# Loading x and the gate weights of a recurrence in two parts of two chunk rows each

## The chip, the cores and the metric

The kernel runs on one core of a Trainium2 chip. The metric is the device time of one execution in microseconds. Three executions of the kernel before took 1618.48, 1618.99 and 1623.41 us; their median is 1618.99 us. One further execution, taken by the hardware profiler, took 1615.84 us, and all rows below are from it.

## The reference

`x` has 16 batch rows of 512 steps and 512 features; four layers are added to it one after the other, each as `x = x + layer(x, cond)`. All is float32.

- Layer 0 is a wavelet transform with a gate on every coefficient. Since the gate is the same for all of them, `v + inverse(gate * forward(v))` is `v * (1 + gate)`, and with the outer sum x becomes `x * (2 + gate)`. The gate depends on `cond` alone.
- Layer 1 is a recurrence over the 512 steps: `h = tanh(x_t @ Wx + b + h @ Wh)`, with `h` of 512 features for 16 batch rows. The next x is `x + h`.
- Layer 2 has a forget gate, an input gate and a candidate, each a product of x with a 512 x 512 matrix; the two gates go through a sigmoid and are divided by their sum, and two running sums and products over the steps follow.
- Layer 3 is a product of x with `base + A B`, where the factors A and B (rank 8 for each batch row) are made from `cond` through a layer norm, a gelu layer and a layer of 8192 columns. With the outer sum the matrix is `base + 2 * identity + A B`.

```python
h_next = jnp.tanh(xw_t + h_prev @ Wh)
forget_gate = jax.nn.sigmoid(jnp.einsum('bsd,hd->bsh', input_seq, W_f) + b_f)
layer = base_layer[None, :, :] + jnp.einsum('bdr,bkr->bdk', x_a, x_b)
out = jnp.einsum('btc,bco->bto', x, layer)
```

## The kernel before

The features lie on 128 partitions in `KC` = 4 chunks. The kernel has three parts: an opening (gate of layer 0, first loads), the recurrence, and a loop over the 16 batch rows for layers 2 and 3.

The recurrence runs over `NBLK` = 64 blocks `n` of `T` = 8 steps `s`. Its order on TensorE (PE), ScalarE (ACT), VectorE (DVE) and SyncE (SP) is the order in which the code is written; nothing is rearranged. In each step

- PE multiplies the last `h` with `wh_sb` (16 products, `accumulate`, L417), and then does other products that do not depend on `h`: the x products of the next block (`inputs`), a part of the rank factors of layer 3 (`layer_part`, L380), or a part of an early gate of layer 2 (`early_gate`, L465);
- ACT takes the tanh of four column groups (L609), and DVE transposes each of them into the next `h` (L610);
- DVE then does one smaller thing: in steps 0 to 3 it multiplies a quarter of the x of block `n + 2` by the gate of layer 0 (`gated`, L178: each quarter takes some steps and all four chunk rows of the loaded tile `xb`), in steps 4 to 7 it adds `h` to x (L622). One piece of an early gate (L489 to L500) may follow;
- ACT issues transfers behind the four tanh: in even steps the second half of a row of the layer 3 weights (`rest`, up to about block 16), in steps 1 and 3 of blocks 0 to 7 one load of a gate weight or of `base`, and in step 5 the x of block `n + 3` (L159) into the single buffer `xb`;
- after that, in steps 7, 0 and 2, ACT copies the bias into a PSUM bank of a coming block (`begin`, L214), and the sigmoid of an early gate may follow.

The x of block `n + 3`, loaded in block `n`, is first read by DVE in step 0 of block `n + 1`. The first early gate begins in block 2; `SETS` and `PARTS` set the order of the others, in the order of weight chunks 2, 3, 0, 1. `base_sb` is read at the end of block 12, where DVE adds twice the identity to its diagonal blocks (L666, four operations), and then only after the recurrence. SP issues the first halves of the layer 3 weights, the stores of the early gates and the rank factors. At the end of a block `end_layer` adds the bias of a rank factor (L395) and stores it; in step 0 of block 1 it makes the hidden layer of layer 3 instead (DVE L399 and L400, then a gelu on ACT, L401).

A DMA issue of SP or ACT also waits until an earlier transfer, some eight before it, is complete, since the semaphores of the transfers are used in turn.

Of the kernel before, what the change touches and what calls it, by code (L numbers as in the profile page):

```python
# [35 lines left out]
P = 128  # L36
B, S, D = 16, 512, 512
KC = D // P
R = 8

T = 8
NBLK = S // T
# [3 lines left out]
G = len(PAIRS)  # L46
# [37 lines left out]
def kernel(  # L84
# [21 lines left out]
    nc = tc.nc  # L106
    PSUM = bass.MemoryType.PSUM

    def chunks(w):
        return w.rearrange("(k p) n -> p k n", p=P)  # L110
# [12 lines left out]
    wf_sb = keep.tile([P, KC, D], F32)  # L123
    wi_sb = keep.tile([P, KC, D], F32)
    wc_sb = keep.tile([P, KC, D], F32)
    base_sb = keep.tile([P, KC, D], F32)
# [13 lines left out]
    xpool = rnn.enter_context(tc.tile_pool(name="xpool", bufs=3))  # L140
# [13 lines left out]

    bias_sb = rw.tile([P, KC, BP], F32)

    def load_x(n, pool=xpool, tag="xb", engine=nc.sync):
        xb = pool.tile([P, KC, T, B], F32, tag=tag, name=f"xb_{n}", bufs=1)
        engine.dma_start(  # L159
            out=xb.rearrange("p k t b -> p k (t b)"),  # L160
            in_=xT[:, n * T : (n + 1) * T, :].rearrange("(k p) t b -> p k (t b)", p=P),
        )
        return xb

    H = G // 2
# [14 lines left out]
    def new_x1(n):  # L180
        return xpool.tile([P, KC, G, 2, B], F32, tag="x1", name=f"x1_{n}")
# [14 lines left out]
    def new_bank(n, i, name):  # L196

        return ps_r[i][n % 2].tile([P, G, P], F32, tag="pre", name=f"{name}_{n}_{i}")
# [25 lines left out]
    with tc.tile_pool(name="ps_pre", bufs=1, space=PSUM) as ps_pre:  # L224
# [15 lines left out]
        xb = load_x(2)  # L240
# [108 lines left out]


    rest = []
    chunk_sb = []

    def load_chunk():
# [14 lines left out]
    def layer_part(i, k):  # L369

        if k == 0:
            layer_part.ps = ps_p.tile([P, P], F32, tag="pf", name=f"pf_{i}")
            if i:
                which, r = LAYERS[i]
                layer_part.bias = w2pool.tile([P, P], F32, tag="b2", name=f"b2_{i}", bufs=2)
                row = (bias_a, b2b)[which][r].rearrange("(j o p) -> j o p", j=KC, o=1)
                nc.sync.dma_start(out=layer_part.bias, in_=row.to_broadcast([KC, BP, P]))
        columns, src = (straight, hT3) if i else (tile_columns, aeT)
        for j in range(KC):
            nc.tensor.matmul(  # L380
                layer_part.ps[j * BP : (j + 1) * BP, :],
                src[:, k, :],
                columns(chunk_sb[i * KC + k], j),
                start=(k == 0),
                stop=(k == KC - 1),
                skip_group_check=True,
            )
        load_chunk()
# [27 lines left out]
    def accumulate(pre, g, j, lhsT, w):  # L416
        nc.tensor.matmul(  # L417
            pre[PLACE[g][0]][j * BP : (j + 1) * BP, PLACE[g][1], :],
            lhsT,
            tile_columns(w, j),  # L420
            start=False,
            stop=False,
            skip_group_check=True,
        )

    def inputs(n, i, pre):

        g, k = divmod(i, KC)
        for j in range(KC):
            accumulate(  # L430
                pre, g, j, xs[n][:, k, PAIRS[g][0] // 2].rearrange("p t b -> p (t b)"), wx_sb[:, k, :]
            )
# [122 lines left out]

    BEGINS = {T - 1: 0, 0: 1, 2: 2}

    pre, nxt = banks
    for _ in range(AHEAD):
        load_chunk()  # L560
# [4 lines left out]
    for n in range(NBLK):  # L565
        ahead = []
        if n + 2 < NBLK:
            xs.append(new_x1(n + 2))
        for s in range(T):
            odd = s % 2  # L570
            waiting = len(rest)
            g = next(i for i, pair in enumerate(PAIRS) if s in pair)
            for k in range(KC):
                for j in range(KC):
                    accumulate(pre, g, j, h_prev[:, k, :], wh_sb[:, k, :])
            if n == 0 and s < G - 1:
                for i in range((s + (s > 0)) * KC, (s + 2) * KC):
                    inputs(0, i, pre)

            if n + 1 < NBLK:  # L580
                if n == 1 and s in LATE:
                    for i in range(*LATE[s]):
                        inputs(n, i, pre)
                for i in range(*SHARE[n][s]):
                    inputs(n + 1, i, nxt)
            if s in LAYER_STEPS[n]:
                layer_part(n, LAYER_STEPS[n].index(s))
            if s in PARTS[n]:
                early_gate(made, n * T + s)
                made += 1  # L590
            if (n, s) == (NBLK - 1, T - 1):


                first_layer = [
                    new_bank(NBLK, i, "pl").rearrange("p g f -> p (g f)") for i in range(NBANK)
                ]
                first_layer.append(ps_q.tile([P, D], F32, tag="pg", name="pl_3"))
                make_layer(*first_rows, first_layer)
            a = apool.tile([P, P], F32, tag="a", name=f"a_{n}_{s}")

            h = h_out[s]
            if odd:
                turned, h_prev = h[:, :, :BP], h[:, :, B:]
            else:
                turned, h_prev = h[:, :, B:], h[:, :, :BP]
            bank, place = PLACE[g]
            for c in range(KC):
                at = slice(c * BP, (c + 1) * BP)
                nc.scalar.activation(a[:, at], pre[bank][:, place, at], AF.Tanh)  # L609
                nc.vector.transpose(turned[:, c, :], a[:, at])  # L610
            if n == 0 and s < G:

                gated(nc.vector, xs[1], x1, (0, 2, 1, 3)[s])
            if n == 0 and s == G - 1:
                opening.close()
                x2pool = ctx.enter_context(tc.tile_pool(name="x2pool", bufs=1, side="right"))
                x2 = x2pool.tile([P, KC, B, S], F32)
            if s == max(PAIRS[g]):
                t0, t1 = PAIRS[g]
                step = t1 - t0  # L620
                at = slice(n * T + t0, n * T + t1 + step // abs(step), step)
                nc.vector.tensor_tensor(  # L622
                    x2[:, :, :, at].rearrange("p k b t -> p k t b"),
                    xs[n][:, :, t0 // 2, :, :],
                    turned.rearrange("p k (t b) -> p k t b", t=2),
                    ALU.add,
                )
            elif n + 2 < NBLK:
                gated(nc.vector, xs[n + 2], xb, s)
            if (n, s) == (1, 1):  # L630

                nc.scalar.activation(probe, g2[:, 0, :1], AF.Sigmoid)
            if waiting and (odd == 0 or n == 0):
                rest.pop(0)()
            if s in (1, 3) and n < 2 * KC:


                i = 2 * n + s // 3
                if i < 3 * KC:
                    m, which = divmod(i, 3)  # L640
                    w_sb, w = ((wf_sb, wfT), (wi_sb, wiT), (wc_sb, wcT))[which]
                    j = (KC - 2, KC - 1, 0, 1)[m]
                    at = slice(j * P, (j + 1) * P)
                    nc.scalar.dma_start(out=w_sb[:, :, at], in_=chunks(w)[:, :, at])
                else:
                    k = i - 3 * KC
                    nc.scalar.dma_start(out=base_sb[:, k, :], in_=base[k * P : (k + 1) * P, :])
            if s == G + 1 and n + 3 < NBLK:
                xb = load_x(n + 3, engine=nc.scalar)
            if s in BEGINS:  # L650
                if s < T - 1 and 0 < n < NBLK - 1:
                    nxt.append(begin(n + 1, BEGINS[s]))
                elif s == T - 1 and n + 2 < NBLK:
                    ahead.append(begin(n + 2, BEGINS[s]))
            if (n, s) == (1, 0):

                end_layer(0)

            for _ in range(1 if n < NBLK - 2 else 2):
                do_pieces(n * T + s)  # L660
        if 0 < n < len(LAYERS):
            end_layer(n)
        if n == 2 * KC + 4:
            for k in range(KC):
                diag = base_sb[:, k, k * P : (k + 1) * P]
                nc.vector.scalar_tensor_tensor(diag, ident, 2.0, diag, ALU.mult, ALU.add)  # L666
        if n == FIRST - 1:
            turn_bias()
        if n == NBLK - 4:
            at = w2pool.tile([P, P], F32, tag="b2", name="at_0", bufs=2)  # L670
            bt = w2pool.tile([P, D], F32, tag="w2", name="bt_0", bufs=AHEAD)
            first_rows = load_layer(0, at, bt)
        pre, nxt = nxt, ahead
# [197 lines left out]
```

## Time and profile before

| what | value |
|---|---|
| median of three executions | 1618.99 us (1618.48 to 1623.41) |
| the profiled execution | 1615.84 us, span 1614.1 us |
| opening, to the first tanh | 16.7 us |
| recurrence with layer 3 weight loads, blocks 0 to 16 | 16.74 to 255.56, DMA share 0.48, 132 GB/s |
| recurrence, blocks 17 to 63 | 255.56 to 908.10, DMA share 0.12, 34 GB/s |
| layers 2 and 3 | 908.10 to 1614.10 |
| PE busy | 1603.6 us, 99% of the span |
| DVE / ACT / GpSimd busy | 1132.3 / 424.9 / 172.6 us |
| granted TensorE clock | 1.000 |
| x loads on ACT's queue | 61 of 256 KB, issue 0.374 to 0.412 us |
| l3w loads on ACT's queue | 64 of 128 KB |
| weight loads on ACT's queue | 12 of 256 KB for the gates, 4 of 256 KB for base |

A row of the order of time is: start in us, duration, engine, line, operation, out<-in with sizes, xcount, and in brackets how long the engine had been idle before and who released it. Rows that follow each other without a gap are merged under their count. `ACTq` and `SPq` are the sequencers, where issues of DMAs show. `PEld` is the weight load of PE. A row of the waits is: engine, what it waited with, whom it waited for, microseconds in total, number, the longest. A row of stretches is: from:to, length, then busy microseconds and instructions in brackets for PE, PEld, DVE, ACT and GpSimd, the granted clock, the mean share of the 16 DMA engines, and GB/s. PE's busy time is modelled for pipelined products, so its 99% does not mean that it works at its peak.

### The profile page before, as it was taken

The page shows a single profiled execution, that of the slowest core. Times are in us where ns is not written, and L with a number is a line of the kernel's source. Part 1 is how long each engine was busy: PE and PEld are TensorE (multiplying, and loading weights), DVE is VectorE, ACT ScalarE, POOL GpSimd, SP SyncE. Part 2 cuts the span into 40 slices and gives each one's busy share as a digit, 9 for nine tenths or more (in the row PEclk, how much of TensorE's full clock was granted, in tenths as well). Part 3 has the DMA queues.
Part 4 walks back from the last instruction along what each step waited for, and adds up shares of the span by engine and source line. Part 5 has one row for each costly group of instructions (what it writes and reads, how often), then busy time and mean ns, then how long its engine had stood idle before and what let it go on. Part 6 is the DMA issues. An engine that isn't in the chain of part 4 may idle for free.

```text
span 1614.1 us, 67901 instructions
## 1 busy us (share of the span) xinstructions
PE 1603.6 (99%) x29328; PEld 1146.0 (71%) x29328; DVE 1132.3 (70%) x3618; ACT 424.9 (26%) x2484; POOL 172.6 (11%) x145
## 2 busy tenths in 40 slices
PE   9999999999999999999999999999999999999998
PEld 6888888888888888888888655555555555555564
DVE  4555655565556666666665798888888888988887
ACT  3333333333333333333333211111111111111111
POOL 0000000000000000000000022222222222222222
PEclk9999999999999999999999999999999999999999
DMA  7554431111111111111111101111111111111111
GB/s 228 148 147 128 121 105 46 36 31 36 37 37 37 37 37 37 37 37 31 37 39 30 29 21 43 33 43 39 43 40 44 44 46 39 31 44 47 37 44 58
DMA packets 128085, 88.11 MB, mean 55 GB/s; under 512 B 22645, under 2 KB 116633, under 8 KB 127785
## 3 DMA queue, kind: packets, MB, share of 16 engines
q1 hardware_dynamic: 79152, 55.05, 11.1%
q10 hardware_dynamic: 48632, 28.73, 6.2%
q8 instruction: 229, 3.75, 1.0%
q14 instruction: 72, 0.58, 0.1%
HBM read 55.67 MB, written 28.07 MB: 52 GB/s over the span
## 4 chain that ended last, share of the span: by engine, by line
PE 96%; DVE 2%; DMA 1%; issue 0%; SPq 0%; ACT 0%; ACTq 0%; DVEq 0%
PE pre L417 41%; PE po L756 13%; PE pg L465 13%; PE pf L700 9%; PE pc L700 9%; PE pi L700 9%; PE pf L380 1%; PE pl_layer L535 1%; DVE s L718 1%; DMA wh_sb<-in_wh_dram 1%; PE pl_last L756 0%; DMA xb<-in_xT_dram 0%; DVE s L726 0%; DVE s L730 0%; PE po_last L756 0%
## 5 line engine op out<-in xcount | busy, mean ns | idle before, releaser
L417 PEld LDWEIGHTS pre<-wh_sb,h_out 128*32 128x32 f32 x16384 | 466.7, 110 | 146.6 <-DVE h_out L610 143.4
L417 PE MATMUL pre<-wh_sb,h_out 128*32 128x128 f32 x16384 | 560.6, 273 | 2.4 <-DVE h_out L610 1.1
L610 DVE STREAM_TRANSPOSE h_out<-a 128x32 f32<-128x32 f32 x2048 | 264.6, 187 | 347.4 <-ACT a L609 345.9
L609 ACT ACTIVATE a<-pre 128x32 f32<-128x32 f32 x2048 | 238.0, 203 | 573.4 <-PE pre L417 572.7
L417 PE MATMUL pre<-wx_sb,x 128*32 128x128 f32 x8192 | 285.9, 273 | 1.0 <-DMA wx_sb<-in_wx_dram 0.5
L417 PEld LDWEIGHTS pre<-wx_sb,x 128*32 128x32 f32 x8192 | 239.0, 110 | 2.1 <-DMA wx_sb<-in_wx_dram 1.5
L756 PE MATMUL po<-wx_sb,x 128*128 128x512 f32 x480 | 209.0, 592 | 0.1
L756 PEld LDWEIGHTS po<-wx_sb,x 128*128 128x128 f32 x480 | 91.0, 190 | 111.6 <-issue 105.7
L700 PE MATMUL pf<-x,wf_sb 128*128 128x352 f32 (+3 forms) x512 | 165.3, 466 | 0.3 <-DVE x L622 0.3
L700 PE MATMUL pc<-x,wc_sb 128*128 128x352 f32 (+3 forms) x512 | 163.7, 463 | 1.3 <-DVE i L722 1.3
L700 PE MATMUL pi<-x,wi_sb 128*128 128x352 f32 (+3 forms) x512 | 163.6, 462 | 0.0
L718 DVE RECIPROCAL s<-s 128x368 f32<-128x368 f32 (+2 forms) x64 | 152.2, 2378 | 2.2
L700 PEld LDWEIGHTS pf<-x,wf_sb 128*128 128x128 f32 x512 | 96.0, 190 | 68.4 <-issue 15.8
L736 POOL TENSOR_TENSOR s<-s,f 128x512 f32<-128x512 f32 x63 | 86.5, 1374 | 509.9 <-DVE s L730 504.1
L700 PEld LDWEIGHTS pc<-x,wc_sb 128*128 128x128 f32 x512 | 97.2, 190 | 57.5 <-DVE i L722 1.9
L700 PEld LDWEIGHTS pi<-x,wi_sb 128*128 128x128 f32 x512 | 97.3, 190 | 55.9
L622 DVE TENSOR_TENSOR x<-x,h_out 128x128 f32<-128x128 f32 x256 | 101.2, 395 | 18.9 <-DMA wi_sb<-in_wiT_dram 0.2
L751 ACT COPY osb<-po 128x512 f32<-128x512 f32 x60 | 35.1, 585 | 263.4 <-PE po L756 144.9
L683 POOL MEMSET zero<- 128x1 f32 x1 | 0.1, 98 | 907.5 <-DVE wx_sb L539 907.5
L717 DVE SCALAR_TENSOR_TENSOR s<-f,i 128x368 f32<-128x368 f32 (+2 forms) x64 | 34.7, 543 | 88.1 <-ACT i L716 88.1
L716 ACT ACTIVATE f<-pf,vec_sb 128x368 f32<-128x368 f32 (+2 forms) x64 | 35.7, 558 | 215.2 <-PE pf L700 160.6
L465 PE MATMUL pg<-x,wc_sb 128*32 128x512 f32 (+1 forms) x640 | 84.2, 581 | 0.0
(113 smaller groups left out, 1270.8 us busy)
## 6 DMA issues: line engine op xcount, KB each, us to landing
out_dram<-osb SPq DMA_DIRECT2D x63, 256.0 KB
xb<-in_xT_dram ACTq DMA_DIRECT2D x61, 256.0 KB
w<-in_l3w_dram SPq DMA_DIRECT2D x72, 128.0 KB
w<-in_l3w_dram ACTq DMA_DIRECT2D x64, 128.0 KB
early<-ef SPq DMA_DIRECT2D x39, 128.0 KB
early<-ei SPq DMA_DIRECT2D x39, 128.0 KB
f<-early SPq DMA_DIRECT2D x16, 96.0 KB
i<-early SPq DMA_DIRECT2D x16, 96.0 KB
```

The lines of the kernel that those rows point to most:

```text
L417: nc.tensor.matmul(pre[PLACE[g][0]][j * BP : (j + 1) * BP, PLACE[g][1], :], lhsT, tile_columns(w, j), start=False, stop=False, skip_group_ ...
L465: nc.tensor.matmul(ps[c * BP : (c + 1) * BP, :].rearrange("p (b t) -> p b t", **shape), w[:, k, j * P + c * BP : j * P + (c + 1) * BP], x2 ...
L609: nc.scalar.activation(a[:, at], pre[bank][:, place, at], AF.Tanh)
L610: nc.vector.transpose(turned[:, c, :], a[:, at])
L622: nc.vector.tensor_tensor(x2[:, :, :, at].rearrange("p k b t -> p k t b"), xs[n][:, :, t0 // 2, :, :], turned.rearrange("p k (t b) -> p k ...
L700: nc.tensor.matmul(p[:, te:], w_sb[:, k, j * P : (j + 1) * P], x2[:, k, b, te:], start=(k == 0), stop=(k == KC - 1),)
L716: nc.scalar.activation(gate[:, new], p[:, new], AF.Sigmoid, bias=col(bias, j))
L717: nc.vector.scalar_tensor_tensor(s[:, new], f[:, new], EPS, i[:, new], ALU.add, ALU.add)
L718: nc.vector.reciprocal(s[:, new], s[:, new])
L736: engine.tensor_tensor(s, s, f, ALU.add)
L751: nc.scalar.copy(osb, po)
L756: nc.tensor.matmul(po, x3[:, k, t * P : (t + 1) * P], layer[:, k, :], start=(k == 0), stop=(k == KC - 1))
```

## The change

The x of a block is loaded in two transfers of two chunk rows each (128 KB), the first issued in step 5 as before, the second in step 7. Each of the twelve gate weight loads becomes two transfers of two chunk rows each, and `base` is loaded in eight transfers of two chunk rows and half of the columns; one of these 32 parts is issued in steps 1 and 3 of each of blocks 0 to 15. Before, the 16 loads went out in steps 1 and 3 of blocks 0 to 7. The four operations on the diagonal of `base` move from the end of block 12 to the end of block 56. All loads stay on ACT's queue, behind the four tanh of the step and, in step 7, ahead of the bias copy.

```diff
-    def load_x(n, pool=xpool, tag="xb", engine=nc.sync):
+    def new_x(n, pool=xpool, tag="xb"):
+
         xb = pool.tile([P, KC, T, B], F32, tag=tag, name=f"xb_{n}", bufs=1)
-        engine.dma_start(
-            out=xb.rearrange("p k t b -> p k (t b)"),
-            in_=xT[:, n * T : (n + 1) * T, :].rearrange("(k p) t b -> p k (t b)", p=P),
+        return xb, (
+            xb.rearrange("p k t b -> p k (t b)"),
+            xT[:, n * T : (n + 1) * T, :].rearrange("(k p) t b -> p k (t b)", p=P),
         )
+
+    def load_x(n, pool=xpool, tag="xb"):
+        xb, (to, source) = new_x(n, pool, tag)
+        nc.sync.dma_start(out=to, in_=source)
         return xb
...
+    def halves_of(to, source):
+
+        half = to.shape[1] // 2
+        return [
+            lambda at=at: nc.scalar.dma_start(out=to[:, at], in_=source[:, at])
+            for at in (slice(0, half), slice(half, 2 * half))
+        ]
...
+    x_parts, weight_parts = [], []
+    for j in (KC - 2, KC - 1, 0, 1):
+        at = slice(j * P, (j + 1) * P)
+        for w_sb, w in ((wf_sb, wfT), (wi_sb, wiT), (wc_sb, wcT)):
+            weight_parts.extend(halves_of(w_sb[:, :, at], chunks(w)[:, :, at]))
+    for k in range(0, KC, 2):
+        for n in range(2):
+            weight_parts.extend(halves_of(base_sb[:, k : k + 2, n * D // 2 : (n + 1) * D // 2],
+                                          chunks(base)[:, k : k + 2, n * D // 2 : (n + 1) * D // 2]))
...
-            if s in (1, 3) and n < 2 * KC:
-
-
-                i = 2 * n + s // 3
-                if i < 3 * KC:
-                    m, which = divmod(i, 3)
-                    w_sb, w = ((wf_sb, wfT), (wi_sb, wiT), (wc_sb, wcT))[which]
-                    j = (KC - 2, KC - 1, 0, 1)[m]
-                    at = slice(j * P, (j + 1) * P)
-                    nc.scalar.dma_start(out=w_sb[:, :, at], in_=chunks(w)[:, :, at])
-                else:
-                    k = i - 3 * KC
-                    nc.scalar.dma_start(out=base_sb[:, k, :], in_=base[k * P : (k + 1) * P, :])
+
             if s == G + 1 and n + 3 < NBLK:
-                xb = load_x(n + 3, engine=nc.scalar)
+                xb, load = new_x(n + 3)
+                x_parts.extend(halves_of(*load))
+            for at, parts in (((1, 3), weight_parts), ((G + 1, G + 3), x_parts)):
+                if s in at and parts:
+                    parts.pop(0)()
...
-        if n == 2 * KC + 4:
+        if n == NBLK - 8:
             for k in range(KC):
                 diag = base_sb[:, k, k * P : (k + 1) * P]
                 nc.vector.scalar_tensor_tensor(diag, ident, 2.0, diag, ALU.mult, ALU.add)
```

## The prediction, made before the changed kernel was run

> **What bounds the kernel now.** I read the split of the span by stage first, then the waits, then the recurrence step by step in order of time. By stage, TensorE is the only engine without gaps. The change touches only the first two stages, up to 908 us:
>
> ```profile
> 16.74:255.56 238.82, 238.00 (x7577) 208.52 (x7573) 133.77 (x763) 84.10 (x605) 0.00 (x0) 1.00 0.48 132
> 255.56:908.10 652.54, 651.43 (x19404) 536.41 (x19398) 391.05 (x2120) 227.25 (x1669) 0.00 (x0) 1.00 0.12 34
> ```
>
> The columns are PE, its weight loads, VectorE (DVE), ScalarE (ACT), GpSimd, granted clock, DMA share, GB/s. The waits say that the recurrence is a ring: ACT waits for PE, DVE for ACT, PE for DVE; x is hardly waited for.
>
> ```profile
> ACT a L609 <- PE pre L417: 572.7, 509, 2.1
> ...
> DVE h_out L610 <- ACT a L609: 345.9, 507, 2.7
> ...
> PEld pre L417 <- DVE h_out L610: 143.4, 255, 0.8
> ...
> DVE x L178 <- DMA xb<-in_xT_dram: 1.1, 2, 0.6
> ```
>
> The third view is order of time on ACT, steps 5, 6, 7 of block 16 and step 0 of block 17; x is issued in step 5:
>
> ```profile
> 250.32 0.20 ACT L609 ACTIVATE a<-pre 128x32 f32<-128x32 f32 x1 [1.27 <-PE pre L417]
> 250.41 0.39 ACTq L159 DMA_DIRECT2D xb<-in_xT_dram  x1
> ...
> 252.06 0.47 ACT L609 ACTIVATE a<-pre 128x32 f32<-128x32 f32 x4 [1.28 <-PE pre L417]
> 253.81 0.46 ACT L609 ACTIVATE a<-pre 128x32 f32<-128x32 f32 x4 [1.28 <-PE pre L417]
> 254.31 0.38 ACT L214 COPY pre<-bias_sb 128x256 f32<-128x256 f32 x1
> 255.56 0.47 ACT L609 ACTIVATE a<-pre 128x32 f32<-128x32 f32 x4 [0.87 <-PE pre L417]
> ```
>
> From tanh to tanh the steps take 1.74, 1.75, 1.75 us: the one that holds the x issue is no longer. The ring is a metronome. Block 0's first tanh starts at 16.74 and block 63's at 896.17: 879.43 us for 63 blocks. An undisturbed block (18, 20, 21 and most later ones) takes 13.91, and 63 of them 876.33. So **3.1 us is all that the loads can cost today** in this stage. Of it 2.42 lies in six blocks (0, 1, 5, 11, 12 and 29: 14.17, 14.28, 14.49, 14.17, 14.47, 14.30), 0.68 is spread.
>
> **The change, part by part.** *Issues on ACT.* 61 x loads become 122 and 16 weight loads 32: 77 more issues of 0.33 us (the 128 KB l3w rows) to 0.39 (the whole x), 25 to 30 us of ACT's queue. Each stands behind a step's four tanh, with 1.28 us idle before the next. In step 7 the bias copy L214 is queued behind the new issue: in step 0 of block 16, which has an issue in that place, the copy starts 0.44 after the first tanh (241.63 to 242.07), without one 0.32 (255.56 to 255.88). So it comes 0.12 later, out of 0.87 idle. The sigmoids of the early gates stand in steps 6, 0, 2 and 4, where the change issues nothing (one, at 61.74, in a step 1 that has a weight issue today too). Cost 0; without that cover it would be 61 x 0.37 = 22.6. SP's and GpSimd's instructions and PE's order are unchanged; an early gate gets a second wait on PE, for the other half of its weight, whose shortest lead is step 3 of block 3 (64.4) to block 4 (73.1): 8.7 us against at most 3.8 for a load (below). Cost 0.
>
> *When the second half of x lands.* DVE's first gating operation (L178) of the next block reads all four chunk rows, so it now waits for a transfer issued in step 7, not 5. That operation with DVE's next transposes, and the DMA rows of the whole x:
>
> ```profile
> 256.20 0.25 DVE L178 TENSOR_TENSOR x<-xb,g 128x128 f32<-128x128 f32 x1
> 257.52 0.49 DVE L610 STREAM_TRANSPOSE h_out<-a 128x32 f32<-128x32 f32 x4 [1.07 <-ACT a L609]
> ```
> ```profile
> 252.25:252.50 0.25, 0.25 (x17) 0.25 (x12) 0.21 (x2) 0.25 (x4) 0.00 (x0) 1.00 1.11 336
> ...
> 252.75:253.00 0.25, 0.25 (x20) 0.25 (x12) 0.22 (x2) 0.00 (x0) 0.00 (x0) 1.00 0.34 86
> 253.00:253.25 0.25, 0.25 (x18) 0.25 (x12) 0.22 (x1) 0.00 (x0) 0.00 (x0) 1.00 0.00 0
> ```
>
> Issued at 250.41, moving from 251.4 (the quarter from 251.25 has 10 GB/s, none before it any) to 253.0: 2.6 us for 256 KB. A half takes at least 1.0 + 131 KB / 336 GB/s = 1.4 and at most those 2.6; I take 1.8 (1.0, and half of the 1.6 of movement). Issued at 253.81 + 0.09 = 253.90, it lands at 255.7, due at 256.20 (2.30 after the issue). A late landing first eats slack: behind the gating DVE has 0.25 us and, in other blocks, one piece of an early gate of 0.42 to 0.55 before the next transposes at 257.52. So tanh is reached only from about 2.8 us after the issue on (3.4 without a piece). Even the bound of 2.6 costs nothing: 0 over blocks 17 to 60.
>
> *The same in blocks 1 to 16, with the l3w loads.* In block 8 the whole x is issued at 138.17, and with three l3w parts of 128 KB beside it the queues are empty only at about 142.0: at most 3.8 us. The second half would be issued at 141.66, and the half microseconds from 142.0 carry 33, 0 and 14 GB/s, so the quiet row is nearer: 1.8 to 2.6, cost 0. The other end, 3.8 everywhere, is 0.4 us a block without a piece and 1.0 with one: 16 x 0.4 = 6.4 to 16 us.
>
> *Block 0.* Step 7 there issues an l3w part first (29.11, 0.35), so the half goes at 29.5, into a DMA share of 0.69 to 0.99. It is due at 31.57; behind it DVE has L399 and L400 (to 32.38), for which ACT waits with the gelu L401 (32.48), and the tanh of step 1 is queued behind that on ACT. This chain has no slack. With 2.6 us the half is 0.5 late: **+0.5**, once (0 with 1.8; +1.7 with 3.8).
>
> *The four operations on base* (0.87 us together, 198.72 to 199.59) move from the end of block 12 to that of block 56. There DVE is free from 812.09 to 812.92: +0.04, bounds 0 and 0.87. I credit nothing for their old place, because the stall there is PE's:
>
> *Stalls of PE for "issue".* The long step at the end of block 12 is this:
>
> ```profile
> 199.05 0.73 PE L417 MATMUL pre<-wh_sb,h_out 128*32 128x128 f32 x17 [0.28 <-issue]
> ```
> ```profile
> q8 instruction: 229, 3.75, 1.0%
> ```
> ```profile
> 198.75:199.00 0.25, 0.02 (x3) 0.00 (x0) 0.25 (x3) 0.00 (x0) 0.00 (x0) 1.00 0.07 18
> ```
>
> The instruction queue (packets, MB, share of 16 engines) moves 16.4 KB packets, each 1% x 16 x 1614 / 229 = 1.13 us of one engine; a share of 0.07 is one engine of sixteen, at 12 to 20 GB/s. It runs from 198.0, when x and an l3w part have just ended, to 199.25, and PE stands meanwhile. Blocks 5, 11 and 29 show the same kind of gap; the four cost 0.58 + 0.26 + 0.56 + 0.39 = 1.79. If a block of instructions waits behind a bulk load, halves shorten that wait; if not, nothing changes. Ends 0 and -1.79 (+1.8 if new collisions take their place); I take half: **-0.9**.
>
> The Trainium skill ("DMA: Bandwidth & Descriptors", Queues, rings and completion order) says that each DMA engine takes turns between queues packet by packet; by that a fetch would run beside the load, its size would not matter, and the term would be 0, not -0.9. The same page (Anatomy of one DMA, and Rules for kernel authors) gives a transfer about 2.0 us fixed plus bytes over 436 GB/s, and so asks for few large ones: against this change. It puts the half at an estimated 2.3 us, just on the due time, and 61 more fixed parts would be 122 us if they were on the path; the sum stays, as they run beside the ring.
>
> **Sum.** -0.9 + 0.5 + 0.04 = -0.4: the profiled execution of 1615.84 (span 1614.1 and 1.7 around it) becomes 1615.4. The median shown is 3.15 above that execution, so I predict 1618.6.
>
> **Rivals.** *B, slower: the second half is late in blocks 1 to 16.* For it: one step less lead than two, the l3w traffic, the 3.8 us bound. Against it: the near-empty queues after step 7 of block 8. It passes 0.3% (4.9 us, about what a measurement of this kernel tells from no change) when the halves land some 0.3 us past the slack in each of the 16. Price 6.4 to 16: 1625 to 1635. *C, faster: the runs without a profile hold more of the instruction stalls.* For it: the 3.15 us. All of that, the 1.79 and the 0.68: 1613.4. Against it: nothing shows what the 3.15 are. *D, hidden anyway:* no stall goes and block 0 has room: 1619.0. *E, slower: ACT's queue becomes the bound in step 7.* One issue lasted 0.82 beside SP's (at 27.35); with the copy's shift that is at the edge of 0.87. The 22.6 above gives 1641.6; against it, step 5 shows no trace of its issue.
>
> **How the numbers follow.** Forecast A 0.53, D 0.23, B 0.12, C 0.07, E 0.05. A's own range is 1616.5 to 1621.5: the stalls' ends, block 0's ends, and the 1618.48 to 1623.41 of the runs shown. The range with 8 in 10, 1614.5 to 1623.5, reaches into C and to the edge of B and E. A and D are within 0.3%: 0.76; C faster 0.07; B and E slower 0.17.
>
> **What would show it.** Right: blocks 17 to 62 still take 13.91; L178 waits for x little or not at all after block 1; the step from 0 to 1 in block 1 grows by about 0.5; fewer gaps of PE for "issue". Wrong: steps 0 of blocks 1 to 16 longer than 1.8, with the next transposes held up behind L178; or step 7 longer everywhere, which would be ACT.

## The result, and the profile after

The changed kernel takes 1622.57 us (median of 22 executions, 1618.65 to 1626.96), the kernel before 1619.51 (22 executions, 1616.52 to 1623.41). The ratio is 1.0019, with a 95% interval of 1.0012 to 1.0026: slower by 3.1 us, where the prediction had 0.4 us faster. That is within the 0.3% that the prediction took for the limit of a measurement, but 22 executions of each resolve it.

The waits of the changed kernel (engine, line, what it waited for: us in total, times, longest), the tanh now on L633, the transposes on L634, the gating on L183:

```profile
ACT a L633 <- PE pre L431: 576.6, 510, 3.5
DVE h_out L634 <- ACT a L633: 330.8, 488, 4.2
...
PEld pre L431 <- DVE h_out L634: 146.0, 254, 0.8
...
DVE x L183 <- DMA xb<-in_xT_dram: 14.2, 17, 2.3
...
ACT hT L415 <- DVE got L414: 3.2, 1, 3.2
```

The ring is what it was. New is the fourth line: before, the gating waited twice for x, 1.1 us in total; now 17 times, 14.2 us. The fifth is new in its length, and happens once.

From the first tanh to the last, by blocks, from the starts of the tanh on ACT (us; an undisturbed block takes 13.91):

| blocks | before | changed |
|---|---|---|
| 0 | 14.17 | 15.08 |
| 1 | 14.28 | **17.37** |
| 2 and 3 | 27.89 | 29.39 |
| 4 to 16 | 182.48 | 182.39 |
| 17 to 62 | 640.61 | 641.31 |
| sum | 879.43 | 885.54 |

The profiled execution of the changed kernel took 1623.54 (span 1621.8), 7.7 more than that of before. 6.1 of it is in this table. Another 1.55 lies ahead of the first tanh (18.29 instead of 16.74), where the two kernels issue the same instructions; what that is comes at the end. Nor is all of the table a late half: block 0's excess is in its first step (2.97 us instead of 1.78), which lies in a piece of half clock, and of the 1.5 us in blocks 2 and 3 only 0.13 stands behind a late gating; 0.67 is step 3 of block 3, where PE stalls 0.34 us for "issue". So the profile tells where to look, and the ratios tell how much.

**Block 1.** The rows of ACT, then of DVE, around the start of block 1 in the changed kernel (start, duration; in brackets the idle time before and what ended it):

```profile
31.57 0.35 ACTq L381 DMA_DIRECT2D w<-in_l3w_dram  x1
...
31.96 0.46 ACTq L362 DMA_DIRECT2D xb<-in_xT_dram  x1
...
37.29 0.26 ACT L415 ACTIVATE hT<-got 128x64 f32<-128x64 f32 x1 [3.21 <-DVE got L414]
```
```profile
36.36 0.29 DVE L183 TENSOR_TENSOR x<-xb,g 128x128 f32<-128x128 f32 x1 [2.25 <-DMA xb<-in_xT_dram]
36.57 0.31 DVE L413 STREAM_TRANSPOSE got<-pf 128x128 f32<-128x128 f32 x1
36.91 0.29 DVE L414 TENSOR_TENSOR got<-got,vec_sb 128x128 f32<-128x128 f32 x1
37.67 0.49 DVE L634 STREAM_TRANSPOSE h_out<-a 128x32 f32<-128x32 f32 x4 [0.47 <-ACT a L633]
```

The second half of x, issued at 31.96 behind an l3w part, lets the gating start at 36.36, 4.40 us later. Elsewhere the gating starts 0.64 after the first tanh of a block, here at 34.01 (33.37 + 0.64): 2.35 late. L413, L414 and the gelu L415 (L399, L400 and L401 before) follow one another without room, the tanh of step 1 stands behind the gelu, and so steps 0, 1 and 2 take 4.08, 2.64 and 2.05 instead of some 1.74 each. In half microseconds (PE, its weight loads, DVE, ACT, POOL, granted clock, DMA share, GB/s):

```profile
35.50:36.00 0.50, 0.00 (x0) 0.00 (x0) 0.00 (x0) 0.00 (x0) 0.00 (x0) 1.00 0.21 70
36.00:36.50 0.50, 0.00 (x0) 0.00 (x0) 0.14 (x1) 0.00 (x0) 0.00 (x0) 1.00 0.03 10
...
37.50:38.00 0.50, 0.40 (x8) 0.27 (x12) 0.33 (x4) 0.48 (x6) 0.00 (x0) 0.59 0.00 0
38.00:38.50 0.50, 0.50 (x20) 0.47 (x16) 0.33 (x3) 0.50 (x1) 0.00 (x0) 0.50 0.00 0
...
40.50:41.00 0.50, 0.50 (x16) 0.47 (x12) 0.49 (x5) 0.32 (x2) 0.00 (x0) 0.50 0.05 8
41.00:41.50 0.50, 0.50 (x28) 0.48 (x20) 0.00 (x0) 0.00 (x0) 0.00 (x0) 1.00 0.20 68
```

TensorE has nothing to multiply for 2.2 us, and when it starts again its clock is granted at half until 41.0: the batch of 32 products takes 1.93 us instead of 1.08. So in this execution the late half costs twice, once as the wait and once as some 1.2 us more in steps 1 and 2. The second cost is a matter of chance. The record lists a mean granted clock for each execution: 8 of the changed kernel's 22 stand at 1.000, which leaves no room for 3.4 us at half (0.0011 of the span), and the median of these 8 is still 1621.69 us (the kernel before at 1.000: 1618.09, at the end).

**The later blocks.** In blocks 17 to 61 the gating is 0.75 to 1.29 us late in each of the eleven blocks 18, 22, 26 and so on to 58, and at most 0.82 in the 34 others, most of them 0.00 to 0.2. In six of the eleven the lateness reaches the tanh, 1.12 us together; in the others DVE's room swallows it. Block 26 of the changed kernel, whose half was issued at 386.08, on DVE and in quarter microseconds:

```profile
388.04 0.49 DVE L634 STREAM_TRANSPOSE h_out<-a 128x32 f32<-128x32 f32 x4 [0.57 <-ACT a L633]
389.65 0.29 DVE L183 TENSOR_TENSOR x<-xb,g 128x128 f32<-128x128 f32 x1 [1.11 <-issue]
389.86 0.42 DVE L510 TENSOR_TENSOR ei<-ei,es 128x256 f32<-128x256 f32 x1
390.19 0.48 DVE L634 STREAM_TRANSPOSE h_out<-a 128x32 f32<-128x32 f32 x4
```
```profile
388.75:389.00 0.25, 0.25 (x20) 0.25 (x16) 0.00 (x0) 0.00 (x0) 0.00 (x0) 1.00 0.55 160
389.00:389.25 0.25, 0.25 (x20) 0.25 (x12) 0.00 (x0) 0.00 (x0) 0.00 (x0) 1.00 0.07 20
389.25:389.50 0.25, 0.25 (x18) 0.25 (x12) 0.00 (x0) 0.00 (x0) 0.00 (x0) 1.00 0.07 20
```

The gating starts 3.57 us after the issue and pushes the next transposes up against L510 (no idle time before them); the view names no releaser here, but the half's last packet ends at 389.12, 0.53 us before. In the last two quarters shown a share of 0.07, one engine of sixteen, is still at work. Of the packets in them 17 are SP's, and 5 are the last of x. In blocks 2 to 16 the gating is more than 0.3 us late in eight blocks, by up to 1.64 (block 9); 0.8 us of it reaches the tanh.

### The profile page after: what moved, and what is told of

Same layout as the page of the kernel before. It is cut to its first block, busy times and chain, and to the rows that moved or that the text cites. A ratio compares the mean times of both kernels' runs of the same rounds, so it can differ in the third digit from the quotient of the medians.

```text
span 1621.8 us, 67977 instructions
## 1 busy us (share of the span) xinstructions
PE 1607.6 (99%) x29328; PEld 1146.2 (71%) x29328; DVE 1134.5 (70%) x3618; ACT 424.9 (26%) x2484; POOL 172.6 (11%) x145
## 4 chain that ended last, share of the span: by engine, by line
PE 95%; DVE 2%; DMA 2%; issue 1%; ACT 0%; SPq 0%; ACTq 0%; DVEq 0%
PE pre L431 41%; PE po L772 13%; PE pg L479 12%; PE pf L716 9%; PE pc L716 9%; PE pi L716 9%; DMA xb<-in_xT_dram 1%; PE pf L394 1%; PE pl_layer L549 1%; DVE s L734 1%; PE pl_last L772 0%; DMA wx_sb<-in_wx_dram 0%; DVE s L742 0%; DVE s L746 0%; PE po_last L772 0%
## 5 line engine op out<-in xcount | busy, mean ns | idle before, releaser
L634 DVE STREAM_TRANSPOSE h_out<-a 128x32 f32<-128x32 f32 x2048 | 264.4, 186 | 332.9 <-ACT a L633 330.8
L633 ACT ACTIVATE a<-pre 128x32 f32<-128x32 f32 x2048 | 238.1, 203 | 577.6 <-PE pre L431 576.6
L479 PE MATMUL pg<-x,wf_sb 128*32 128x512 f32 (+1 forms) x640 | 83.8, 582 | 0.0
```

Source lines behind the costliest of these rows:

```text
L479: nc.tensor.matmul(ps[c * BP : (c + 1) * BP, :].rearrange("p (b t) -> p b t", **shape), w[:, k, j * P + c * BP : j * P + (c + 1) * BP], x2 ...
```

## The experiments

Diffs are against the changed kernel, except where said. All ratios are to the kernel before, run on the same chip, with 95% intervals; 0.001 is 1.6 us.

### Which part of the change costs: x, the weights, or ACT's queue

x_only takes back the parts of the weights and base and keeps the halves of x; w_only keeps the parts and loads x whole in step 5; x_46 issues the halves one step earlier; x_from1 loads only block 0's x whole.

```diff
  x_only (the lines of the kernel before for weights and base put back)
-            for at, parts in (((1, 3), weight_parts), ((G + 1, G + 3), x_parts)):
+            for at, parts in (((G + 1, G + 3), x_parts),):
  w_only
-                x_parts.extend(halves_of(*load))
+                nc.scalar.dma_start(out=load[0], in_=load[1])
  x_46
-            if s == G + 1 and n + 3 < NBLK:
+            if s == G and n + 3 < NBLK:
...
-            for at, parts in (((1, 3), weight_parts), ((G + 1, G + 3), x_parts)):
+            for at, parts in (((1, 3), weight_parts), ((G, G + 2), x_parts)):
  x_from1
-                x_parts.extend(halves_of(*load))
+                if n == 0:
+                    nc.scalar.dma_start(out=load[0], in_=load[1])
+                else:
+                    x_parts.extend(halves_of(*load))
```

> Only x is loaded in two parts (steps 5 and 7); the weights of the gates and base are loaded whole as before, and the diagonal of base is made at the end of block 12. Theory L (the second part of x lands after DVE wants it): the whole loss of the change is here, 1.0012 to 1.0026 of before, and the profile shows DVE waiting for xb for 8 us or more, against 1.1 before. Theory W (the loss is in the weight parts, which load the queues up to block 15): 0.9996 to 1.0004, with a few blocks late at most.

> Only the weights and base are loaded in parts; x is loaded whole in step 5. Theory L: 0.9995 to 1.0005 of before, DVE waits for xb about 1 us as before, and block 1 takes 14.3 or less. Theory W: 1.0012 to 1.0026, and blocks 2 to 15 hold the excess.

> The changed kernel with the parts of x issued in steps 4 and 6 instead of 5 and 7, one step or 1.74 us more lead for each. Theory L: the profile's second parts were up to 1.3 us late (2.35 in block 1), so all but that of block 1 come in time and block 1 keeps about 0.6: 0.9995 to 1.0006 of before. Theory W, and a third, Q (77 more issues on ACT's queue cost by themselves): no better than the changed kernel, 1.0012 to 1.0026.

> The changed kernel, but the x that block 0 issues is loaded whole in its step 5. In the profile of the changed kernel steps 0 and 1 of block 1 took 3.2 us too long, and steps 0 and 1 of all later blocks together 2.0. Theory L with the start as its main part: 2.5 to 3 us less than the changed kernel, 1.0000 to 1.0009 of before. Theory L with the later blocks as its main part: 1.0010 to 1.0022.

| kernel | median us | ratio | gating's waits for x in the profile |
|---|---|---|---|
| x_only | 1623.09 | 1.0029 [1.0020, 1.0039] | 14.2 us, 20 times |
| w_only | 1618.56 | 0.9999 [0.9989, 1.0008] | 0.6 us, once |
| x_46 | 1618.93 | 0.9993 [0.9984, 1.0001] | 1.7 us, 3 times |
| x_from1 | 1619.82 | 1.0005 [0.9996, 1.0013] | 11.7 us, 18 times |

The loss is in the halves of x; the parts of the weights cost nothing that shows. (x_only lies above the 1.0026 that theory L allowed it, x_46 just below its 0.9995.) x_46 has the same number of issues on ACT as the changed kernel and one step more lead, and the loss is gone: so it is the lead, not ACT's queue. Block 0's half alone is worth about 0.0014 (1.0019 less 1.0005).

### Is it the two parts, or the lead?

x_55 issues both halves in step 5, x_whole7 the whole x in step 7.

```diff
  x_55
-            for at, parts in (((1, 3), weight_parts), ((G + 1, G + 3), x_parts)):
-                if s in at and parts:
-                    parts.pop(0)()
+            for at, parts in (((1, 3), weight_parts), ((G + 1, G + 1), x_parts)):
+                for step in at:
+                    if s == step and parts:
+                        parts.pop(0)()
  x_whole7
-            if s == G + 1 and n + 3 < NBLK:
+            if s == G + 3 and n + 3 < NBLK:
...
-                x_parts.extend(halves_of(*load))
+                nc.scalar.dma_start(out=load[0], in_=load[1])
```

> The changed kernel with both halves of x issued in step 5, one right after the other: as many transfers and waits as the changed kernel, no later issue. Theory S (the issue two steps later is what costs): 0.9993 to 1.0005, block 1 at 13.8 to 14.4, hardly any wait of the first gating for x. Rival D (two parts cost as such: a second fixed time, twice the issues, a second wait): 1.0015 to 1.0030, with waits of the first gating for x or longer steps 5.

> The changed kernel with x in one piece, issued in step 7: the same lead as the second half has, twice its bytes. Theory S: the whole x takes 2.6 us instead of the 2.4 of a half, and with an instruction packet in the way up to 1.5 more; the first gating is then 0.3 us late in every block, which the blocks with a piece of an early gate behind it absorb, and 1 us or more late in one block in four: +5 to +11 us, ratio 1.0030 to 1.0070, above the changed kernel. Rival D (the two parts are what costs): at or below 1.0005, since there are no parts of x. Rival W2 (the late landing is absorbed and the changed kernel loses elsewhere): about the 1.0019 of the changed kernel or less.

x_55: 1618.88 us, 0.9997 [0.9987, 1.0006], no wait of the gating for x in the list. x_whole7: 1629.77 us, 1.0065 [1.0053, 1.0078], in the upper half of what the late landing foretold. Two parts as such cost nothing, the lead costs all. The group of the gating in x_whole7 (busy, mean ns, then the idle time before it and what ended it):

```profile
L183 DVE TENSOR_TENSOR x<-xb,g 128x128 f32<-128x128 f32 x256 | 66.4, 261 | 53.9 <-DMA xb<-in_xT_dram 53.7
```

54 us of waits cost 10 us. In x_whole7 the gating of blocks 17 to 61 starts at least 0.44 us late everywhere, by 0.70 on the mean outside the blocks 18, 22, 26 ..., and 29 of those 34 blocks lose nothing on the tanh; the eleven blocks of the beat are 1.19 to 2.20 late and lose 7.35 us of the 8.4. That is the room behind the gating that the prediction had read from DVE's rows.

### Block 0 by itself, and the quiet blocks by themselves

```diff
  x_blk0
-                x_parts.extend(halves_of(*load))
+                if n > 0:
+                    nc.scalar.dma_start(out=load[0], in_=load[1])
+                else:
+                    x_parts.extend(halves_of(*load))
  x_quiet
-                x_parts.extend(halves_of(*load))
+                if n < 16:
+                    nc.scalar.dma_start(out=load[0], in_=load[1])
+                else:
+                    x_parts.extend(halves_of(*load))
  x_skip7 (halves in block 0 alone, as x_blk0, and)
-            if waiting and (odd == 0 or n == 0):
+            if waiting and (odd == 0 or (n == 0 and s < G + 3)):
```

> Only block 0 loads its x as two halves, in its steps 5 and 7; from block 1 on x goes whole in step 5; gate weights and base in parts as in the changed kernel. Theory S (the start: the half issued in step 7 of block 0 stands behind an l3w part, and nothing behind the first gating of block 1 has slack): block 1 takes about 17.3 us instead of 13.9 to 14.3, and all of it stays: +1.6 to +3.2 us, ratio 1.0010 to 1.0020, which is the changed kernel (1.0019) less the later blocks. Rival M (most of the loss is in the later blocks): within 0.0005 of 1. Rival N (what is lost in block 1 is won back later, since the loads then have more time): block 1 long, and the ratio still within 0.0005 of 1.

> Blocks 0 to 15 load x whole in step 5, halves in steps 5 and 7 only from block 16 on; gate weights and base in parts as in the changed kernel. Theory S (from block 17 on a half is late only where an instruction packet lies on one of the 16 engines in the 2.4 us after its issue, about one block in four, by 0.1 to 0.8 us on the steps): +1 to +2.5 us, ratio 1.0004 to 1.0014; block 1 takes 13.8 to 14.3; the long blocks are 22, 26, 30, 34 and so on, each with an instruction packet in the window. Rival P (a half issued in step 7 is late as such, packet or not): nearly all of 45 blocks a little long, 0.05 to 0.3 each, 2 to 13 us. Rival Z (nothing happens in the quiet stage): within 0.0003 of 1.

> Only block 0 loads x in halves, as in x_blk0, but the l3w part that ACT issues in step 7 of block 0 just ahead of the second half is left for the next step that has none. Theory T (the half of block 0 takes 4.4 to 4.65 us because 128 KB of l3w stand ahead of it on the same queue): the gate comes 0.4 us earlier by the earlier issue and some 0.4 to 1.0 us by the free queue, block 1 takes 15.0 to 16.6 us, ratio 1.0003 to 1.0010. Rival U (the DMA engines are full of SP's transfers and the queue does not matter): issue to gate stays above 4.2 us, block 1 at 17 or more, ratio 1.0010 to 1.0018.

x_blk0: 1621.20 us, 1.0014 [1.0004, 1.0025], block 1 at 17.39 us; it is not won back. x_quiet: 1622.32 us, 1.0014 [1.0004, 1.0023], at the upper end of what was expected; block 1 at 14.17. In its profile the gating is 0.78 to 1.68 late in all eleven blocks of the beat, which lose 3.47 us; the 34 others are at most 0.67 late and lose nothing. So the loss has two places, about as large as each other: block 1, and one quiet block in four. That x_blk0 and x_quiet add up to 1.0028 and x_only shows 1.0029, but the changed kernel 1.0019 and x_from1 (which has all that x_quiet has) 1.0005, is within what the intervals allow; how large each share is in the changed kernel stays open by about 1 us.

x_skip7: 1619.53 us, 0.9997 [0.9989, 1.0006], less than was expected. Where the half of block 0 does not stand behind an l3w part, its row on ACT and that of the gating are:

```profile
32.41 0.38 ACTq L362 DMA_DIRECT2D xb<-in_xT_dram  x1
```
```profile
35.76 0.29 DVE L183 TENSOR_TENSOR x<-xb,g 128x128 f32<-128x128 f32 x1 [0.76 <-DMA xb<-in_xT_dram]
```

and in x_blk0, with the l3w part at 32.51 ahead of it:

```profile
32.90 0.52 ACTq L362 DMA_DIRECT2D xb<-in_xT_dram  x1
```
```profile
37.55 0.29 DVE L183 TENSOR_TENSOR x<-xb,g 128x128 f32<-128x128 f32 x1 [2.13 <-DMA xb<-in_xT_dram]
```

3.35 us from issue to gating against 4.65: 1.3 us for the 128 KB ahead on the queue. The gating is then 0.86 late, block 1 takes 14.83, and the clock stays at 1.00 there.

### Why every fourth block: the instruction packet

A half moves in 272 packets, 17 for each of the 16 engines if they are shared evenly. In x_only and x_quiet each half that came more than 0.7 us late had one packet of the instruction queue moving between its issue and its landing. That is a coincidence in time; to make it a test, x_beat issues halves in steps 5 and 7 only in the eleven blocks ahead of the late ones, x_offbeat only in the 33 others.

```diff
  x_beat
-                x_parts.extend(halves_of(*load))
+                if n > 16 and n % 4 == 1:
+                    x_parts.extend(halves_of(*load))
+                else:
+                    nc.scalar.dma_start(out=load[0], in_=load[1])
  x_offbeat: the same with
+                if n > 16 and n % 4 != 1:
```

> Halves in steps 5 and 7 only in the blocks 17, 21, 25 and so on up to 57, eleven in all, before the long blocks 18, 22, 26 ... of the earlier profiles; x whole in step 5 in all others; gate weights and base in parts. Theory I (an instruction packet on one of the 16 engines holds back that engine's share of the half, and the packets meet the halves in a beat of four blocks): all of the loss of the quiet stage is here: 7 to 11 of the eleven gates that follow are 0.7 us or more late, blocks 17 to 62 take 2.0 to 3.5 us more than 640.5, ratio 1.0005 to 1.0018. Rival P (a half issued in step 7 is late in any block with like chance): a quarter of the loss, 0.6 to 0.9 us, ratio within 0.0006 of 1, and two or three of the eleven gates that late.

> The opposite: halves in steps 5 and 7 in all blocks from 18 on but 17, 21, 25 and so on, 33 blocks; those load x whole in step 5, as do the blocks before 17. Theory I: 33 blocks with the late issue and hardly any loss: no gate more than 0.8 us late, blocks 17 to 62 within 0.4 us of 640.5, ratio 0.9993 to 1.0005. Rival P: three quarters of the loss, 1.8 to 2.6 us, ratio 1.0008 to 1.0018.

| kernel | halves | gating late | lost on the tanh by it | median us | ratio |
|---|---|---|---|---|---|
| x_beat | 11 | 0.67 to 1.76, mean 1.20 | 2.89 us, in 8 blocks | 1622.07 | 1.0014 [1.0005, 1.0023] |
| x_offbeat | 33 | 0.00 to 0.60, mean 0.11 | 0 | 1619.04 | 0.9989 [0.9981, 0.9998] |

Eleven late issues cost what 45 do, and three times as many in the other blocks cost nothing (x_offbeat's ratio is even below the 0.9993 that was expected). Block 22 of x_beat, whose half is issued at 327.91: DVE, the queues in the 4 us from the issue (packets, MB, share of 16 engines), and quarter microseconds:

```profile
329.87 0.49 DVE L634 STREAM_TRANSPOSE h_out<-a 128x32 f32<-128x32 f32 x4 [0.47 <-ACT a L633]
331.57 0.29 DVE L183 TENSOR_TENSOR x<-xb,g 128x128 f32<-128x128 f32 x1 [1.21 <-DMA xb<-in_xT_dram]
```
```profile
q10 hardware_dynamic: 272, 0.13, 12.2%
q8 instruction: 1, 0.02, 1.9%
```
```profile
328.66:328.91 0.25, 0.25 (x20) 0.25 (x13) 0.25 (x2) 0.11 (x1) 0.00 (x0) 1.00 0.30 66
...
329.16:329.41 0.25, 0.25 (x20) 0.25 (x15) 0.25 (x1) 0.00 (x0) 0.00 (x0) 1.00 0.63 188
329.41:329.66 0.25, 0.25 (x12) 0.15 (x5) 0.00 (x0) 0.02 (x1) 0.00 (x0) 1.00 0.69 205
329.66:329.91 0.25, 0.25 (x8) 0.00 (x0) 0.04 (x1) 0.25 (x4) 0.00 (x0) 1.00 0.14 39
329.91:330.16 0.25, 0.25 (x8) 0.02 (x4) 0.25 (x3) 0.25 (x4) 0.00 (x0) 1.00 0.07 8
...
330.66:330.91 0.25, 0.25 (x19) 0.25 (x14) 0.00 (x0) 0.00 (x0) 0.00 (x0) 1.00 0.05 6
```

A quarter counts the packets that start in it. The instruction packet starts in the first (66 GB/s in it are its 16.4 KB; 1.9% of 16 engines and 4 us are 1.2 us of one engine) and lasts from 328.81 to 330.00. The x packets of the quarters that follow up to 329.91 are 29, 94, 107 and 25, together 255, all over by 329.82; then 4, 4, 5 and 4 trickle in: the last 17, one engine's share, at a DMA share of 0.05 to 0.08. They follow one another from 329.99 to 330.86, that is from the moment that the instruction packet ends. A block of x_offbeat, issued at 533.71, has its packet too, but after x:

```profile
536.08 0.25 DVE L183 TENSOR_TENSOR x<-xb,g 128x128 f32<-128x128 f32 x1
```
```profile
534.71:534.96 0.25, 0.25 (x19) 0.25 (x13) 0.25 (x2) 0.00 (x0) 0.00 (x0) 1.00 0.41 115
534.96:535.21 0.25, 0.25 (x18) 0.25 (x13) 0.24 (x1) 0.00 (x0) 0.00 (x0) 1.00 0.94 270
535.21:535.46 0.25, 0.25 (x12) 0.13 (x6) 0.00 (x0) 0.02 (x1) 0.00 (x0) 1.00 0.47 135
535.46:535.71 0.25, 0.25 (x8) 0.00 (x0) 0.04 (x1) 0.25 (x4) 0.00 (x0) 1.00 0.28 70
535.71:535.96 0.25, 0.25 (x8) 0.03 (x4) 0.25 (x3) 0.25 (x4) 0.00 (x0) 1.00 0.00 0
```

All of x is in by 535.71, 2.0 us after the issue (the 70 GB/s of that quarter are mostly the instruction packet, which starts at 535.62), and the gating starts on its due time. That the packet and the late share lie on the same engine is read from these counts and times, not from a view of single engines.

SP's stores are the other suspect, and the packets' times answer it. In the six profiles with halves in step 7 (changed, x_only, x_quiet, x_from1, x_beat, x_offbeat) blocks 17 to 61 gate 224 of them. The 64 that have an instruction packet under way 1.4 us after the issue are all late, by 0.50 to 1.76 us. The 112 without one between 0.5 and 1.6 us after it are at most 0.30 late, although 34 of these have 284 to 462 packets of SP's queue beside them. Stores alone don't make a half late; beside an instruction packet they add to it (mean lateness 1.33 us with 544 or 545 packets of SP's queue, 0.93 without).

### A version without the loss

x_only46 has the weights as before and the halves of x in steps 4 and 6.

```diff
  against x_only
-            if s == G + 1 and n + 3 < NBLK:
+            if s == G and n + 3 < NBLK:
...
-            for at, parts in (((G + 1, G + 3), x_parts),):
+            for at, parts in (((G, G + 2), x_parts),):
```

> The changed kernel without the parts of the gate weights and base (those as before, base taken up at the end of block 12), and with the halves of x in steps 4 and 6. If the second half's due time is all that costs, the due time is now 4.1 us after the issue and no gate is late: 0.9985 to 1.0003, waits of the first gating for x under 2 us. If the parts of the weights had a gain of their own, this is above x_46 (0.9993); if they cost something, below it.

1618.27 us, 0.9992 [0.9983, 1.0000]; the gating waits for x once, 0.3 us. With x_46 (0.9993) and x_offbeat (0.9989) it stands at the edge of a gain of 1 to 2 us, and only the interval of x_offbeat lies below 1. All three beat the changed kernel; none beats the kernel before by an amount that is worth more than a hint.

## Why the prediction was wrong

The measured 1622.57 us lies in the wide range (1614.5 to 1623.5), above A's own (1616.5 to 1621.5), and on the other side of no change than the forecast.

- **When the second half of x lands**, the step that failed. It took 1.8 us for the half, due at 2.30, and said that even 2.6 would cost nothing. Its 0 over blocks 17 to 60 was 1.1 us in the profile of the changed kernel and 3.5 in that of x_quiet (2.3 by the ratio). The 1.8 is right for the data of a good half: in x_offbeat they move from 1.0 to at most 2.0 us after the issue. Two things were missing. The gating does not start when the last packet lands: in block 37 of x_whole7 the data end between 2.25 and 2.5 us and the gating starts at 2.82. So a good half is usable at about 2.1 to 2.4, on the due time (2.38) with no reserve. And a landing can be held up: the 2.6 was one clean transfer, taken for a bound, while the profile of before held 229 instruction packets of 1.13 us of one engine each, and in block 12 of it the whole x, issued at 194.41, moved until 198.91, 4.5 us, with an instruction packet beside it from 195.64 to 197.68. The halves behind one are usable 3.0 to 4.1 us after the issue. The step's 2.8 to 3.4 us, from which tanh is reached, stands roughly (3.2 to 3.6 in the profiles): in x_beat block 42 loses nothing at 3.37 and block 46 0.16 at the same 3.37, block 22 loses 0.46 at 3.66.
- **The page's estimate** of 2.3 us for a half (the Trainium skill, "DMA: Bandwidth & Descriptors", Anatomy of one DMA, which fits it to transfers issued by GpSimd; these are ACT's) was nearer to the moment of use than the 1.8 from the rows.
- **The page's rule on queues** (the same page, Queues, rings and completion order) is that an engine drains a whole packet of one queue before it turns to the next. The runs agree with it; wrong was what the prediction drew from it, that a fetch runs beside the load and its size does not matter. With 16.4 KB in one packet a turn is 0.9 to 1.9 us in x_beat, 1.1 at the median, and the gating waits for the slowest of sixteen engines.
- **Block 0** was mis-sized: +0.5 with an upper end of +1.7, and 2.3 us in x_blk0. The chain (L399, L400 and the gelu of before) was right. The half took 4.40 to 4.65 us, over the 3.8 that the prediction held for the most, 1.3 of it for the l3w part ahead of it (one profile with it and one without), which the prediction named and did not add: ACT issues such parts in odd steps of block 0 too, not in even steps alone. And TensorE's clock at half after the wait was not thought of.
- **The same in blocks 1 to 16**: cost 0 was forecast, 0.8 us of the changed kernel's profile is there. The quiet row did not hold even where it was taken: the half issued in block 8, which block 9 gates, went out at 148.26, had an instruction packet beside it from 149.45 to 150.83, and was 1.64 late.
- **Issues on ACT**, cost 0: right. In the quiet blocks a half's issue takes as long as that of the whole x (0.37 to 0.39 us), steps 5 and 7 stay at 1.74 to 1.75, and x_55 and x_46 with the same 122 issues lose nothing. The bias copy starts 0.50 after the first tanh in step 7 of block 37 of x_beat, and so it did before (253.81 to 254.31 in the prediction's own rows): no later, where the prediction took 0.12 from step 0.
- **The four operations on base**, +0.04: right as far as seen; block 56 of the changed kernel takes 13.91.
- **Stalls of PE for "issue"**, -0.9: not shown, and read wrongly. The prediction took the share of 0.07 from 198.0 to 199.25 for the instruction queue. In the profile of before that stretch holds no packet of it:

```profile
q10 hardware_dynamic: 27, 0.01, 5.6%
q1 hardware_dynamic: 7, 0.01, 2.0%
```

The 27 are the end of the x of block 12 named above, held up as the halves are now. What makes PE stall there stays open, and nothing says that smaller loads shorten it: steps 2 to 7 of blocks 2 to 16 took 1.6 us over undisturbed ones before, 2.2 in the changed kernel, and 0.9 to 3.8 in the twelve other profiles. x_46, x_only46 and x_offbeat come out at 0.9989 to 0.9993, which would fit -0.9, but two of the intervals reach 1, and x_55 and w_only, which also have smaller loads and no late ones, are at 0.9997 and 0.9999. The prediction asked how long an instruction packet waits for x, not how long x waits for it.
- **Rivals.** B had the mechanism, a late second half, but not its place: it priced all of blocks 1 to 16, and the loss is in block 1 and in the blocks up to 61 that meet an instruction packet. Its price of 6.4 us at the least was too high. E, ACT's queue, falls with x_46 and x_55; C and D with the sign.

## What to carry to other kernels

A load's lead has to cover its slowest engine's share and not the clean transfer: look in the trace of before for what else takes engines (here instruction packets of 1.1 us), add it and the part of a microsecond between the last packet and the first use, and compare the sum with the due time. To see whether a late landing matters, read the room of the engine behind the waiting instruction: here the quiet blocks took 0.8 to 1.2 us of lateness without loss, and lost all beyond. Where one place in a kernel has no such room (a chain into the next stage, or a queue with a load ahead), price it by itself, and bring the load forward there first.

## What the runs showed that was not expected

**Half clock in pieces of 3.4 us.** After waits of 2.1 to 2.2 us TensorE's clock was granted at half in block 1 of the changed kernel, x_only and x_blk0, for 3.4 us (0.59 in the half microsecond from 37.5, then 0.50 up to 41.0, above), and not in x_whole7 after a gap of 2.30 (block 1 takes 16.31 there instead of 17.37), nor in x_skip7 after 0.73. Within a profile all changes of the clock lie on a grid of 3.413 us (17.11, 20.52, 37.59 and 41.00 in the changed kernel). In the three kernels 2.20, 2.11 and 2.09 us without a product fell into the one grid piece before the half clock; of x_whole7's gap 1.94 fell into one piece and the rest into the next. So in block 1 it is the idle time within a piece that fits, not the length of the gap; in the opening pieces with 1.2 us were followed by half clock too. The Trainium skill ("TensorE: Matmul & The Clock Gate", Part 1: The HAM clock gate) gives a free-running window of 3413 ns, which fits the length and the grid; it names an idle window of that length as what lowers the clock, and here shorter gaps were enough.

**The opening is a lottery.** Ahead of the first tanh all these kernels issue the same instructions, yet PE waits for wx_sb 1.59 us in the changed kernel and 0.30 at most in the kernel before:

```profile
17.50 2.36 PE L431 MATMUL pre<-wx_sb,x 128*32 128x128 f32 x40 [1.59 <-DMA wx_sb<-in_wx_dram]
```

In the profiled executions the opening holds none, one or two of those pieces of half clock. Without one, kernels that lose little or nothing to late halves took 1615.84 (before), 1616.44 (x_46) and 1616.88 (x_offbeat); with one, w_only 1618.11 and x_only46 1618.27; with two, x_skip7 1620.52 and x_55 1622.10. This is one reason why the executions of one kernel spread, and not the whole of it. By the mean granted clock that is on record for 93 executions of the kernel before (those beside w_only, x_55 and x_beat), the 25 at 1.000 have a median of 1618.09 us, the 41 at 0.999 one of 1619.62, the 27 below that 1620.28; but the 25 alone run from 1615.36 to 1621.40. Why the profiled execution of before was 3.15 below its median stays open.
